# Token attention's chunks as side work of the two local-attention runs

## The chip, the cores and the metric

The kernel runs on one core of one Trainium2 chip. The metric is the device time of one execution in microseconds (us), from the chip, as the median of several runs; less is better. Engines are named as in the profile: PE (matrix products), PEld (its weight loads), DVE (vector), ACT (scalar), POOL (GpSimd), SP (which only issues DMAs here).

## The reference

The reference is a hybrid network on x of shape 8 x 256 x 128, eight residual stages one after the other, each on the layer-normed x. What matters here are stages 2 to 4:

```python
x = x + _L0_ffn_ref(_layernorm(x), Wqkv, q_scale, k_scale, Wo, ln_g, ln_b, W1, b1, W2, b2)   # stage 2: "local"
x = x + _L0_attn_b_ref(_layernorm(x), Wq, Wk, Wv, Wo, bo)                                      # stage 3: "token"
x = x + _L0_ffn_ref(_layernorm(x), Wqkv, q_scale, k_scale, Wo, ln_g, ln_b, W1, b1, W2, b2)   # stage 4: "local" again, same weights
```

The local stage is six layers of windowed attention (16 heads of 64, windows of 32 that look one window back, rotary tables, l2-normed q and k) and a gated feed-forward. Stages 2 and 4 use the same weights. The token stage is, in the reference's own words:

```python
q = (x @ Wq.T).reshape(N, S, H, hd).transpose(0, 2, 1, 3)   # N, S, D = x.shape; H = 16 heads, hd = 8
k = (x @ Wk.T).reshape(N, S, H, hd).transpose(0, 2, 1, 3)
v = (x @ Wv.T).reshape(N, S, H, hd).transpose(0, 2, 1, 3)
att = jnp.einsum('nqhd,nkhd->nhqk', q, k)
att = jax.nn.softmax(att / jnp.sqrt(jnp.asarray(hd, x.dtype)), axis=3)
```

followed by the product with v and by Wo and bo. In the kernel this stage is written for each row of 128 features as a 16 x 16 table of products, summed over 8 and soft-maxed, on DVE and POOL rather than on PE.

## The kernel before

x is held as 128 features by tokens and cut into four chunks of 512 tokens (`NCH`, `CT`). Between stages the chunks go through DRAM: `k.put(c, ...)` stores chunk c, `k.get(c, ...)` loads it, both issued on SP. One large SBUF tile `big` is divided by hand (`Arena`), and the eight PSUM banks are handed out by strings of bank numbers (`bank("01234")` takes the next of five).

**Local stage** (`LocalBlock`). A unit is one layer of one chunk, so there are 24 units, in the order layer by layer, chunk by chunk. `steps` runs a loop over i; at step i, work of several units is issued, each at a fixed distance: `project` of the pair of heads that comes 7 steps later, `rotate` 6, `prep` 1, `scores` 0, `turn` 2 back, `attend` 3 back. A unit has eight steps. Its feed-forward (`feed`, a generator) is advanced by one piece in each of steps 12 to 19 of the unit, and unit 23, the last, gets its pieces at steps 196 to 203. Scores begin at step 0 and end at step 191: steps -10 to -1 are the fill, steps 192 to 211 the drain. `end(c)` adds the residual and stores chunk c, at steps 179, 187, 195 and 203. `begin(c)` loads, norms and places chunk c for a run: chunk 0 before the loop, chunk 1 from step -10, whose load is issued at the end of that step. `side` is a list of generators that prepare the next layer's weights (`load_qk`, `load_tab`, `load_v`, `load_1`, `load_2`), one piece of each per step. `run` loads the weights of the first layer before the loop.

The whole loop stands inside `manual_schedule()`. Inside such a region each engine issues its instructions in the order in which the program emits them; where they fall among instructions from outside the region is left to the scheduler of the framework. Code outside a region is ordered by that scheduler altogether.

**Token stage** (`TokenAttention`). It is outside any such region. Each of four chunks is a `Chain` with its own place in SBUF and two PSUM banks. `chunk` is a generator: `rows` (norm), and then four tiles of 128 tokens, each in four pieces that end at a `yield`:

- A: the product for q, k, v (L1001) and its copies out of PSUM (ACT L1003, L1004);
- B: q times k on POOL (L1010), then the sum (DVE L1014), the maximum, the difference (L1016, L1018), the exponential (ACT L1019), its sum and reciprocal (L1021, L1022);
- C: the weights times v, on DVE and POOL (both L1026), the sum (DVE L1029) and the division (L1031);
- D: eight scaled copies (ACT L1035), eight products (PE L1038) and the residual (DVE L1040).

`weave` emits chunks 0 and 1 alternately, one piece behind each other, then 2 and 3; the scheduler then moves instructions as it sees fit. Chunk 0 needs only what `end(0)` stored, so some of it stands in the trace before the local run has ended.

The main loop calls the stages in turn: `local.run(depth)` for stages 2 and 4, `TokenAttention(k).run()` for stage 3.

Of the kernel before, what the change touches and what calls it, by code (L numbers as in the profile page):

```python
# [217 lines left out]
class LocalBlock:  # L218


    def __init__(self, k):
        self.k, self.nkb = k, 0
        nc = k.nc
# [52 lines left out]
    def load_v(self, w, l, g):  # L276

        k, P, nc = self.k, self.P, self.k.nc
        v, o = (self.raw(k.a[n][l, :, 4 * g:4 * g + 4], (64, 4, 128), "r" + n) for n in ("wv", "wo"))
        yield  # L280
        wp = k.bank(RING)
        for h in range(4):
            nc.tensor.matmul(wp[:, bass.ts(h, 128)], v[:, h], o[:, h], start=True, stop=True)
        wv = P.tile([128, CT], F32, name="wvo", tag="wvo", bufs=NWV)
        nc.scalar.copy(wv, wp)
        w.v.append(wv)

    def load_1(self, w, l):
        k, P, nc = self.k, self.P, self.k.nc
        w.bias1 = P.tile([128, 6], F32, name="bias1", tag="bias1", bufs=2)  # L290
        for i in (3, 4, 5, 0, 1, 2):
            m, o = (128, 128, 85)[i % 3], 341 * (i // 3) + 128 * (i % 3)
            r = self.raw(k.a["w1"][l, :, o:o + m], (128, m), "rw1")
            yield
            bp = k.bank(RING)
            nc.tensor.matmul(bp[:m, 0:1], r, self.ffc[:, l, 1:2], start=True, stop=True)
# [15 lines left out]
    def values(self, u, p):  # L312
# [6 lines left out]
        for q in range(p % 2 * 2, p % 2 * 2 + 2):  # L319
            vp = k.bank(RING)  # L320
            for w in range(4):
                win = 4 * q + w
                xw = y[:, win // 8, 32 * (win % 8):32 * (win % 8) + 32]
                for h in range(4):
                    nc.tensor.matmul(vp[32 * h:32 * h + 32, bass.ts(w, 128)], xw, wv[:, bass.ts(h, 128)],  # L325
                                     start=True, stop=True)
            nc.scalar.copy(v2[:, 4 * q:4 * q + 4].rearrange("p w f -> p (w f)"), vp)  # L327

    def project(self, u, p):
# [5 lines left out]
        for s in range(2):  # L335
            ps = k.bank(RING)
            k.mm3(ps, u.w.qk[p][:, :, bass.ts(s, 128)], u.xs)
# [52 lines left out]
    def rounded(self, u, p):  # L390
# [8 lines left out]
        u.rs[p // GP] = rs  # L399
        tp = k.bank(RING)  # L400
        nc.tensor.transpose(tp[:, 0:128], u.nr, k.ident)
# [4 lines left out]
    def prep(self, u, p):  # L406

        k, nc, tt, rs = self.k, self.k.nc, u.t[p], u.rs[p // GP]
        rb = k.bank(RING)
        nc.tensor.matmul(rb, self.bsel[:, p % GP], rs, start=True, stop=True)  # L410
# [61 lines left out]
    def turn(self, u, p):  # L472
# [6 lines left out]
        for o in range(2):  # L479
            tp = k.bank(RING)  # L480
            for wg in range(4):
# [30 lines left out]
    def attended(self, u, p):  # L512

        k, nc, ao = self.k, self.k.nc, getattr(u, "ao", None)
        if p == 7:
            tp = k.bank(RING)
# [17 lines left out]
    def feed(self, u):  # L534
        k, P, nc, w = self.k, self.P, self.k.nc, u.w
        assert u.att
        for xc, rb in k.layernorm_in_pieces(P, self.y[u.c][:, :, 0:256], (RING, RING), mid=self.mid):
            if rb is None:
# [7 lines left out]
        for i, m in enumerate((128, 128, 85)):  # L546
            gp = k.bank(RING)
            k.mm3(gp[:m], w.w1[3 + i], xh)
# [5 lines left out]
        for i, m in enumerate((128, 128, 85)):  # L554
            ap = k.bank(RING)
# [4 lines left out]
        acc = k.bank(RING)  # L560
        for i in range(3):
# [5 lines left out]
    def begin(self, c):  # L567
# [3 lines left out]
        yield  # L571
        for xc, rb in k.layernorm_in_pieces(P, xl, (RING, RING)):
            if rb is None:
# [15 lines left out]

    def run(self, depth=DEPTH):  # L590


        NU = depth * NCH
        self.P.restart()
        ws = [Rec(tab=[0, 0], qk=[], v=[], w1=[0] * 6, w2=[]) for _ in range(depth + 1)]
# [3 lines left out]
        self.mid = self.top = None  # L599
        w = ws[0]  # L600
        drain([self.begin(0)] + [self.load_tab(w, 0, n) for n in range(2)] + [self.load_v(w, 0, h) for h in range(4)] +
              [self.load_qk(w, 0, p) for p in range(8)] + [self.load_1(w, 0), self.load_2(w, 0)])
        self.mid, self.top = [], []
        with self.k.tc.manual_schedule():
            self.steps(us, ws, depth)

    def steps(self, us, ws, depth):
        NU, done, feed, side = len(us), [0] * NCH, None, []
        for i in range(-LEAD, 8 * NU + 20):
            def do(what, ahead):  # L610
                n, p = (i + ahead) // 8, (i + ahead) % 8
# [16 lines left out]
            if u:  # L628
                last = u.l + 1 == depth
                if u.c == NCH - 1 and not last:  # L630
                    side.append(self.load_qk(ws[u.l + 1], u.l + 1, p))
                    if p in (4, 5):
                        side.append(self.load_tab(ws[u.l + 1], u.l + 1, p - 4))
            do(self.norms, 6)
# [15 lines left out]
            if 0 <= n < NU and p == 7:  # L650
                u = us[n]
                next(feed)
                done[u.c] += 1
                if u.c == NCH - 1 and u.l + 1 < depth:
                    side += [self.load_1(ws[u.l + 1], u.l + 1), self.load_2(ws[u.l + 1], u.l + 1)]
# [4 lines left out]
            if u and u.c == NCH - 1 and u.l + 1 < depth and p % 2 == 0:  # L660
                side.append(self.load_v(ws[u.l + 1], u.l + 1, p // 2))
            do(self.squares, 7)
# [5 lines left out]
            if p == 0 and 0 <= n < NU:  # L668
# [287 lines left out]
class TokenAttention:  # L956
# [3 lines left out]
    def __init__(self, k):  # L960
        self.k = k
        P = Arena(k.big, TOKW)
        self.chains = [Chain(k, c, TOK[c], TOKB[c]) for c in range(NCH)]
        self.w = k.const(P, "f_w", (128, 384))
# [25 lines left out]
    def chunk(self, ch):  # L990
# [8 lines left out]
        for t in range(4):  # L999
            ps = ch.bank(0)  # L1000
            mm(ps[:, 0:384], ch.xc[:, bass.ts(t, 128)], self.w, start=True, stop=True)  # L1001
            z = ch.tile([128, 3, 128], "z", bufs=2)
            nc.scalar.activation(z.rearrange("p a f -> p (a f)"), ps[:, 0:384], AF.Copy, scale=ch.r[:, t:t + 1])  # L1003
# [349 lines left out]
def hybrid_kernel(ctx: ExitStack, tc: tile.TileContext, a, out, stages=(1, 2, 3, 4, 5, 6, 7, 8), depth=DEPTH):  # L1353
    nc = tc.nc
    k = K(ctx, tc, a)
    runs = [s for s in stages if s < 6] + [6] * (stages[-1] >= 6)
    local = None
    for s in runs:
# [141 lines left out]
```

## Time and profile before

| what | value |
|---|---|
| median of 3 runs | 4365.39 us (4363.03 to 4368.97) |
| the profiled execution | 4360.81 us, span from first to last instruction 4359.0 us |
| granted PE clock, mean | 0.926 |
| busy, of the span | PE 87%, PEld 65%, DVE 85%, ACT 60%, POOL 71% |
| scores of the first local run end | near 2187 us |
| first and last L1010 (POOL) of the token stage | start at 2205.5 and 2327.9 us |
| last store of the token stage | issued at 2362.5 us |
| first scores of the second local run | 2414.4 us |

Times in a trace are counted from the start of the span. A line of the timeline has the start, the duration, the engine, the line of the kernel, the operation and how many were merged; in square brackets stands the idle time before it and what ended it. A line of the groups has the busy time in total, then the mean in ns, and after the second bar the idle time before them. A row of the windows view has the busy time of each engine in a stretch with the number of instructions, then the clock that PE was granted (1.00 is full), the busy share of the DMA engines, and GB/s.

### The profile page before, as it was taken

How to read it: one execution, taken by the hardware profiler on the slowest of the kernel's cores; microseconds unless marked ns; L12 is line 12 of the kernel's file. 1: busy time of each engine (PE TensorE's matmuls, PEld its weight loads, DVE VectorE, ACT ScalarE, POOL GpSimd, SP SyncE). 2: the span in 40 equal slices, each digit the busy share in tenths (PEclk: the TensorE clock that was granted, in tenths of full speed). 3: DMA queues.
4: the chain of work that ended last, by engine and by line, in shares of the span. 5: the costliest groups of instructions: out<-in, count | busy, mean ns of one | idle time of the engine just before them, and what ended most of it. 6: DMA issues, size and time to landing. Idle time of an engine off the chain costs nothing. (4 is left out here: it accounts for less than half of the span.)

```text
span 4359.0 us, 147963 instructions
## 1 busy us (share of the span) xinstructions
PE 3780.3 (87%) x64201; PEld 2852.4 (65%) x64201; DVE 3716.3 (85%) x5687; ACT 2628.5 (60%) x5050; POOL 3077.8 (71%) x1546
## 2 busy tenths in 40 slices
PE   5666679999999999999966899999999999998367
PEld 2222248777878778787744788787787877875144
DVE  6999958888888888888976788888888888897988
ACT  5433347777667676676645676676676767764322
POOL 3656668877778787787566887787787877872433
PEclk7777889999999999999977999999999999998578
DMA  0000023323233233232202332232323323321000
GB/s 19 7 3 16 1 77 78 91 73 89 73 74 89 71 89 76 71 93 71 63 22 67 81 92 74 69 94 72 89 70 76 87 71 90 75 72 47 15 6 10
DMA packets 134900, 272.98 MB, mean 63 GB/s; under 512 B 31020, under 2 KB 68328, under 8 KB 134248
## 3 DMA queue, kind: packets, MB, share of 16 engines
q1 hardware_dynamic: 134248, 263.51, 24.0%
q8 instruction: 504, 8.26, 0.8%
q14 instruction: 148, 1.21, 0.1%
HBM read 49.50 MB, written 6.29 MB: 13 GB/s over the span
## 5 line engine op out<-in xcount | busy, mean ns | idle before, releaser
L367 POOL TENSOR_TENSOR big<-big 128x1024 f32<-128x1024 f32 x384 | 915.8, 2385 | 466.7 <-DMA big<-big 322.6
L368 POOL TENSOR_TENSOR big<-big 128x1024 f32<-128x1024 f32 x384 | 916.5, 2387 | 30.1
L325 PE MATMUL pb<-big 128*32 128x128 f32 x24576 | 748.1, 274 | 2.7 <-DVE big L301 2.7
L325 PEld LDWEIGHTS pb<-big 128*32 128x32 f32 x24576 | 683.0, 111 | 8.5 <-DVE big L301 4.0
L327 ACT COPY big<-pb 128x512 f32<-128x512 f32 x768 | 439.4, 597 | 384.2 <-PE pb L325 381.0
L338 ACT COPY big<-pb 128x512 f32<-128x512 f32 x768 | 437.5, 587 | 276.8 <-PE pb L215 241.7
L414 DVE SCALAR_TENSOR_TENSOR big<-big,pb 128x512 f32<-128x512 f32 x768 | 536.0, 738 | 22.3 <-PE pb L410 22.0
L340 DVE TENSOR_TENSOR big<-pb,big 128x512 f32<-128x512 f32 x768 | 496.4, 677 | 58.6 <-ACT big L338 51.5
L213 PE MATMUL pb<-bigr 128*128 128x512 f32 (+1 forms) x1056 | 453.9, 430 | 9.8 <-DVE big L340 4.3
L469 POOL TENSOR_TENSOR big<-big 128x1024 f32<-128x1024 f32 x192 | 365.6, 1904 | 132.2 <-ACT big L338 54.8
L348 ACT ACTIVATE big<-big 128x512 f32<-128x512 f32 x768 | 444.2, 631 | 0.0
L821 POOL TENSOR_TENSOR big<-big 128x1024 f32<-128x1024 f32 x128 | 305.1, 2396 | 192.1 <-DVE big L820 187.1
L429 PE MATMUL pb<-big 128*32 128x128 f32 x12288 | 421.3, 278 | 6.0 <-DVE big L440 6.0
L215 PE MATMUL pb<-bigr 128*128 128x512 f32 (+1 forms) x1056 | 422.2, 400 | 4.6 <-DVE bigr L299 4.6
L214 PE MATMUL pb<-bigr 128*128 128x512 f32 (+1 forms) x1056 | 420.9, 399 | 1.1 <-POOL bigr L203 1.1
L429 PEld LDWEIGHTS pb<-big 128*32 128x32 f32 x12288 | 316.6, 110 | 142.2 <-issue 91.2
L437 DVE TENSOR_TENSOR pb<-pb,big 128x512 f32<-128x512 f32 x384 | 266.3, 694 | 144.2 <-PE pb L429 142.6
L505 PE MATMUL pb<-big 128*32 128x128 f32 x11520 | 377.9, 276 | 0.2 <-ACT big L485 0.2
L814 PE MATMUL pb<-bigr 128*128 128x512 f32 x512 | 216.1, 538 | 181.3 <-DVE big L820 125.7
L450 ACT ACTIVATE big<-big 128x1024 f32<-128x1024 f32 x192 | 203.7, 1061 | 263.6 <-DVE big L440 261.9
L505 PEld LDWEIGHTS pb<-big 128*32 128x32 f32 x11520 | 325.1, 110 | 48.0 <-issue 25.0
L816 ACT ACTIVATE big<-pb,big 128x1020 f32<-128x1020 f32 x128 | 142.2, 1111 | 282.0 <-PE pb L814 191.1
(270 smaller groups left out, 7450.7 us busy)
## 6 DMA issues: line engine op xcount, KB each, us to landing
big<-big SPq DMA_DIRECT2D x768, 256.0 KB, 3.6
big<-in_wqk SPq DMA_DIRECT2D x96, 128.0 KB, 3.5
big<-x SPq DMA_DIRECT2D x28, 256.0 KB, 2.7
big<-in_c_rot SPq DMA_DIRECT2D x24, 256.0 KB, 5.1
big<-in_wv SPq DMA_DIRECT2D x48, 128.0 KB, 3.6
big<-in_wo SPq DMA_DIRECT2D x48, 128.0 KB, 4.0
big<-big SPq DMA_DIRECT2D x384, 16.0 KB, 2.2
x<-big SPq DMA_DIRECT2D x20, 256.0 KB, 2.5
```

Source lines behind the costliest of these rows:

```text
L213: mm(out, w[:, 0], x[:, 0], start=start, stop=False)
L215: mm(out, w[:, 1], x[:, 0], start=False, stop=stop)
L325: nc.tensor.matmul(vp[32 * h:32 * h + 32, bass.ts(w, 128)], xw, wv[:, bass.ts(h, 128)], start=True, stop=True)
L327: nc.scalar.copy(v2[:, 4 * q:4 * q + 4].rearrange("p w f -> p (w f)"), vp)
L338: nc.scalar.copy(raw[:, s], ps)
L340: nc.vector.tensor_tensor(tt[:, s].rearrange("p (b t) -> p b t", b=2), ps.rearrange("p (b t) -> p b t", b=2), ct, ALU.mult)
L348: nc.scalar.activation(sq, raw[:, s], AF.Square)
L367: nc.gpsimd.tensor_tensor(s4, s4, u.w.tab[1][:, :, None, :].broadcast_to([128, 2, 2, T]), ALU.mult)
L368: nc.gpsimd.tensor_tensor(tt, tt, sw, ALU.add)
L414: nc.vector.scalar_tensor_tensor(kb[:, h, 32:], tt[:, 1], self.hcol[:, h:h + 1], rb, ALU.mult, ALU.mult)
L429: mm(s4[32 * w:32 * w + 32, 2 * wg:2 * wg + 2], qf[:, 32 * win:32 * win + 32], kb[:, :, 32 * win:32 * win + 64].rearrange("p h (o j) -> p ...
L505: mm(u.acc[32 * w:32 * w + 32, bass.ts(wg, 128)], pts[o][:, 32 * win:32 * win + 32], v2[:, win - 1 + o], start=False, stop=(g == 3 and o = ...
```

## The change

Token attention is no longer a stage between the two local runs. Its four chunks become generators that the loop of the local stage advances. Chunks 0 and 1 are advanced by one piece per step from step 192 on (the drain of the first run), chunk 1 four steps later than chunk 0; what is left after step 211 is emitted at the end. Chunks 2 and 3 are advanced by three pieces per step in steps -10 to -3 of the second run (its fill), chunk 3 one piece behind chunk 2. All of this is now inside the two `manual_schedule()` regions.

So that the chunks fit beside the local stage, they lie in other parts of SBUF and use other PSUM banks; z and s have one buffer instead of two; the ring of banks of the local stage is four in the drain and three in the fill; the constants are loaded twice, once for each pair. The first layer's weights of the second run are now loaded during the last layer of the first (`more`), as for any other layer, and not before the second run.

```diff
-TOKW, TOK = 14880, (8880, 18160, 24160, 30160)
+TOKW, TOK = (26016, 38368), (15872, 20944, 28224, 33296)
-TOKB = (("4", "6"), ("5", "7"), ("0", "2"), ("1", "3"))
+TOKB = (("5", "6"), ("4", "7"), ("5", "7"), ("3", "4"))
-RING, SCO, NRM, ACC = "01234", "5", "6", "7"
+RING, RING_B, SCO, NRM, ACC = "01234", "0123", "5", "6", "7"
...
-    def run(self, depth=DEPTH):
+    def run(self, depth=DEPTH, more=False, ahead=(), behind=()):
-        self.P.restart()
...
+        if self.first:
+            ws[0] = self.first
+            for u in us[:NCH]:
+                u.w = ws[0]
+        else:
+            w = ws[0]
+            loads += [self.load_tab(w, 0, n) for n in range(2)] + [self.load_v(w, 0, h) for h in range(4)]
+            loads += [self.load_qk(w, 0, p) for p in range(8)] + [self.load_1(w, 0), self.load_2(w, 0)]
+        drain(loads)
...
+        self.first = ws[depth] if more else None
...
         for i in range(-LEAD, 8 * NU + 20):
+            self.ring = RING_B if i >= 8 * NU and behind else RING_B[:3] if i < -2 and ahead else RING
...
-                if u.c == NCH - 1 and not last:
-                    side.append(self.load_qk(ws[u.l + 1], u.l + 1, p))
+                if u.c == NCH - 1 and (more or u.l + 1 < depth):
+                    side.append(self.load_qk(ws[u.l + 1], (u.l + 1) % depth, p))
...
                 if n + 1 < NCH:
                     side.append(self.begin(n + 1))
                     next(side[-1])
-        assert not side
+            if i < -2:
+                for _ in range(3):
+                    ahead = [g for g in ahead if next(g, ahead) is not ahead]
+            elif i >= 8 * NU:
+                behind = [g for g in behind if next(g, behind) is not behind]
+            else:
+                assert not ahead
+        for f in self.top:
+            f()
+        self.top.clear()
+        drain(side)
+        drain(behind)
...
-            z = ch.tile([128, 3, 128], "z", bufs=2)
+            z = ch.tile([128, 3, 128], "z")
...
-            s = ch.tile([128, 16, 16], "s", bufs=2)
+            s = ch.tile([128, 16, 16], "s")
...
-    def run(self):
-        self.k.nc.scalar.preload_act_table_set("natural_log_exp_and_others")
-        for c in range(0, NCH, 2):
-            weave([self.chunk(ch) for ch in self.chains[c:c + 2]], 1)
+    def chain(self, c, skew):
+        if c % 2 == 0:
+            self.consts(TOKW[c // 2])
+        for _ in range(skew):
+            yield
+        ch = Chain(self.k, c, TOK[c], TOKB[c])
+        yield
+        yield from self.chunk(ch)
...
-            local.run(depth)
-        if s == 3:
-            TokenAttention(k).run()
+            more = s == 2 and runs[runs.index(s) + 1:][:2] == [3, 4]
+            if more:
+                token = TokenAttention(k)
+                first, second = [token.chain(0, 0), token.chain(1, 4)], [token.chain(2, 0), token.chain(3, 1)]
+            local.run(depth, more, () if more else second, first if more else ())
```

More of the change, by code (lines that the diff above doesn't have):

```diff
@@ L221, in __init__ @@
     def __init__(self, k):
-        self.k, self.nkb = k, 0
+        self.k, self.nkb, self.first = k, 0, None
         nc = k.nc
@@ L280, in load_v @@
         yield
-        wp = k.bank(RING)
+        wp = k.bank(self.ring)
         for h in range(4):
@@ L294, in load_1 @@
             yield
-            bp = k.bank(RING)
+            bp = k.bank(self.ring)
             nc.tensor.matmul(bp[:m, 0:1], r, self.ffc[:, l, 1:2], start=True, stop=True)
@@ L319, in values @@
         for q in range(p % 2 * 2, p % 2 * 2 + 2):
-            vp = k.bank(RING)
+            vp = k.bank(self.ring)
             for w in range(4):
@@ L335, in project @@
         for s in range(2):
-            ps = k.bank(RING)
+            ps = k.bank(self.ring)
             k.mm3(ps, u.w.qk[p][:, :, bass.ts(s, 128)], u.xs)
@@ L399, in rounded @@
         u.rs[p // GP] = rs
-        tp = k.bank(RING)
+        tp = k.bank(self.ring)
         nc.tensor.transpose(tp[:, 0:128], u.nr, k.ident)
@@ L408, in prep @@
         k, nc, tt, rs = self.k, self.k.nc, u.t[p], u.rs[p // GP]
-        rb = k.bank(RING)
+        rb = k.bank(self.ring)
         nc.tensor.matmul(rb, self.bsel[:, p % GP], rs, start=True, stop=True)
@@ L479, in turn @@
         for o in range(2):
-            tp = k.bank(RING)
+            tp = k.bank(self.ring)
             for wg in range(4):
@@ L515, in attended @@
         if p == 7:
-            tp = k.bank(RING)
+            tp = k.bank(self.ring)
             for wg in range(4):
@@ L536, in feed @@
         assert u.att
-        for xc, rb in k.layernorm_in_pieces(P, self.y[u.c][:, :, 0:256], (RING, RING), mid=self.mid):
+        for xc, rb in k.layernorm_in_pieces(P, self.y[u.c][:, :, 0:256], (self.ring, self.ring), mid=self.mid):
             if rb is None:
@@ L546, in feed @@
         for i, m in enumerate((128, 128, 85)):
-            gp = k.bank(RING)
+            gp = k.bank(self.ring)
             k.mm3(gp[:m], w.w1[3 + i], xh)
@@ L554, in feed @@
         for i, m in enumerate((128, 128, 85)):
-            ap = k.bank(RING)
+            ap = k.bank(self.ring)
             k.mm3(ap[:m], w.w1[i], xh)
@@ L559, in feed @@
         yield
-        acc = k.bank(RING)
+        acc = k.bank(self.ring)
         for i in range(3):
@@ L571, in begin @@
         yield
-        for xc, rb in k.layernorm_in_pieces(P, xl, (RING, RING)):
+        for xc, rb in k.layernorm_in_pieces(P, xl, (self.ring, self.ring)):
             if rb is None:
@@ L599, in run, with steps @@
         self.mid = self.top = None
-        w = ws[0]
-        drain([self.begin(0)] + [self.load_tab(w, 0, n) for n in range(2)] + [self.load_v(w, 0, h) for h in range(4)] +
-              [self.load_qk(w, 0, p) for p in range(8)] + [self.load_1(w, 0), self.load_2(w, 0)])
+        self.ring = RING
+        loads = [self.begin(0)]
+        if self.first:
[7 more added lines that the diff above has]
+        drain(loads)
         self.mid, self.top = [], []
         with self.k.tc.manual_schedule():
-            self.steps(us, ws, depth)
-    def steps(self, us, ws, depth):
+            self.steps(us, ws, depth, more, list(ahead), list(behind))
+        self.first = ws[depth] if more else None
+    def steps(self, us, ws, depth, more, ahead, behind):
         NU, done, feed, side = len(us), [0] * NCH, None, []
         for i in range(-LEAD, 8 * NU + 20):
+            self.ring = RING_B if i >= 8 * NU and behind else RING_B[:3] if i < -2 and ahead else RING
             def do(what, ahead):
@@ L628, in steps @@
             if u:
-                last = u.l + 1 == depth
-                if u.c == NCH - 1 and not last:
-                    side.append(self.load_qk(ws[u.l + 1], u.l + 1, p))
+                if u.c == NCH - 1 and (more or u.l + 1 < depth):
+                    side.append(self.load_qk(ws[u.l + 1], (u.l + 1) % depth, p))
                     if p in (4, 5):
-                        side.append(self.load_tab(ws[u.l + 1], u.l + 1, p - 4))
+                        side.append(self.load_tab(ws[u.l + 1], (u.l + 1) % depth, p - 4))
             do(self.norms, 6)
@@ L653, in steps @@
                 done[u.c] += 1
-                if u.c == NCH - 1 and u.l + 1 < depth:
-                    side += [self.load_1(ws[u.l + 1], u.l + 1), self.load_2(ws[u.l + 1], u.l + 1)]
+                if u.c == NCH - 1 and (more or u.l + 1 < depth):
+                    side += [self.load_1(ws[u.l + 1], (u.l + 1) % depth), self.load_2(ws[u.l + 1], (u.l + 1) % depth)]
                 if u.l + 1 == depth:
@@ L659, in steps @@
             u, p = do(self.values, 2)
-            if u and u.c == NCH - 1 and u.l + 1 < depth and p % 2 == 0:
-                side.append(self.load_v(ws[u.l + 1], u.l + 1, p // 2))
+            if u and u.c == NCH - 1 and (more or u.l + 1 < depth) and p % 2 == 0:
+                side.append(self.load_v(ws[u.l + 1], (u.l + 1) % depth, p // 2))
             do(self.squares, 7)
@@ L961, in __init__, with consts @@
         self.k = k
-        P = Arena(k.big, TOKW)
-        self.chains = [Chain(k, c, TOK[c], TOKB[c]) for c in range(NCH)]
+    def consts(self, at):
+        k = self.k
+        P = Arena(k.big, at)
         self.w = k.const(P, "f_w", (128, 384))
@@ L1356, in hybrid_kernel @@
     runs = [s for s in stages if s < 6] + [6] * (stages[-1] >= 6)
-    local = None
+    local, first, second = None, (), ()
     for s in runs:
```

## Prediction

> **What bounds the kernel now.** I read the page's slices first (the dip between the two local runs, near half of the span), then the windows view over that dip, the groups of instructions inside it, and the timeline. Windows view; busy us of PE, weight loads, DVE, ACT, POOL, then the granted clock:
>
> ```profile
> 2187.00:2205.00 18.00, 15.54 (x162) 11.03 (x155) 7.89 (x13) 8.80 (x15) 1.90 (x1) 0.89 0.01 2
> 2205.00:2232.00 27.00, 19.59 (x73) 12.17 (x72) 20.75 (x23) 14.31 (x31) 12.86 (x4) 0.81 0.19 59
> 2232.00:2349.00 117.00, 64.21 (x290) 50.90 (x289) 105.08 (x140) 57.19 (x175) 106.09 (x36) 0.70 0.09 29
> 2349.00:2370.00 21.00, 13.44 (x70) 10.11 (x70) 6.33 (x17) 9.39 (x25) 1.99 (x2) 0.66 0.29 87
> 2370.00:2414.40 44.40, 29.84 (x319) 20.66 (x315) 15.52 (x28) 22.36 (x46) 31.20 (x15) 0.82 0.37 93
> ```
>
> The rows are: the local drain, drain plus first token tile, the body of token attention, its tail, and the next local run's fill up to its first scores at 2414.4. In the body DVE is busy 105 and POOL 106 of 117 us: two full engines. Groups there (POOL, DVE, ACT and PE of one tile; 16 tiles):
>
> ```profile
> L1010 POOL TENSOR_TENSOR big<-big 128x2048 f32<-128x2048 f32 x16 | 72.0, 4502 | 23.2 <-ACT big L1003 23.2
> ...
> L1026 POOL TENSOR_TENSOR big<-big 128x1152 f32<-128x1152 f32 x16 | 41.8, 2612 | 1.1 <-ACT big L1019 1.1
> ...
> L1014 DVE TENSOR_REDUCE pb<-big 128x256 f32<-128x2048 f32 x16 | 36.6, 2289 | 3.8 <-POOL big L1010 3.3
> L1029 DVE TENSOR_REDUCE pb<-big 128x128 f32<-128x2048 f32 x16 | 36.5, 2282 | 4.4 <-POOL big L1026 4.2
> ```
>
> A tile needs 4.50 + 2.61 = 7.1 us of POOL. The timeline shows that the present order gets exactly that, one tile per 7.0 us (2247.49 to 2254.49 to 2261.51), POOL without a gap:
>
> ```profile
> 2247.49 4.48 POOL L1010 TENSOR_TENSOR big<-big 128x2048 f32<-128x2048 f32 x1
> 2251.93 2.61 POOL L1026 TENSOR_TENSOR big<-big 128x1152 f32<-128x1152 f32 x1
> 2254.49 4.51 POOL L1010 TENSOR_TENSOR big<-big 128x2048 f32<-128x2048 f32 x1
> 2258.95 2.62 POOL L1026 TENSOR_TENSOR big<-big 128x1152 f32<-128x1152 f32 x1
> 2261.51 4.51 POOL L1010 TENSOR_TENSOR big<-big 128x2048 f32<-128x2048 f32 x1
> ```
>
> So today's cost of the stage is engine work, overlapped across chunks by the scheduler, and the drain already hides the first tile. What the change must beat is 2414.4 - 2187 = 227 us.
>
> **What the change makes of it.** Token instructions now stand inside the two hand-ordered regions, where each engine issues in the order written. Each chunk advances one piece at a time. Call the pieces A (L1001, L1003), B (L1010 to L1022), C (L1026 to L1031), D (L1035 to L1040). No piece of a chunk's next tile is written ahead of D of the last one. A tile alone is then a chain: A 0.85 + 0.57; B 4.50 + 2.29 + 0.42 + 0.40 + 0.41; C 2.61 + 2.28 + 0.28; D 2.43 for eight L1035 and 1.95 to 3.79 for L1038: 19 to 21 us. The trace has one such tile, the first: L1010 at 2205.5, its successor at 2226.0, 20.5 us. Only two chunks are alive at a time, and two strictly serial chains can't reach 7 us per tile even if they never hinder each other (20/2 = 10).
>
> L1038 has two lengths in the timeline, after idle and after other work:
>
> ```profile
> 2254.43 3.79 PE L1038 MATMUL pb<-big 128*128 128x128 f32 x16 [4.10 <-ACT big L1035]
> ...
> 2282.66 1.97 PE L1038 MATMUL pb<-big 128*128 128x128 f32 x16
> ```
>
> *Drain, first tile.* Up to step 195 the order is nearly what the scheduler had: B of chunk 0 starts at 2205. Its L1014 stands behind unit 22's L531 and L587 (3.5 us beside POOL), so it starts at 2212.6 (before: 2211.9). Then Exp, C and D end at 2227; unit 23's norm and chunk 1's rows (L973, L980, L179, 1 us each) stand before the next A on PE: next B at 2232.5.
>
> *Drain, pairs.* Skew 4 puts both chunks in the same piece. Walk, from B of chunk 0 at 0: POOL 0 to 4.5 and 4.5 to 9.0; chunk 1's DVE part of B to 13.2; C's DVE work (1.05 + 2.2 + 0.3, twice) to 16.7 and 20.2; L1035 of chunk 1 to 22.7; L1038 (chunk 0's, cold, ended at 22.9) to 24.9; A 0.9 + 0.6: the next B at 26.4. Three such loops (steps 198 to 209) are 79. Unit 23's feed-forward is written between them: nine matmuls in step 202 stand on PE before A (+2.5), and L531 and L587 in step 203 on DVE before L1014 (+3). Its L203 waits behind two B's on POOL, and its gelu in step 200 falls into ACT's idle time before L1035: nothing; without that gap 4.6 (three L549 of 0.69 and two table loads of 1.28). Together 84.5: 2317. Then chunk 1's last tile is alone: 20, to 2337.
>
> *Handover.* SP is one queue. Region two begins by issuing the load of chunk 1 for its own norm (step -10, before the first token piece); it must wait for chunk 1's store, and chunk 2's load and four constants are queued behind it. Store 2.5, six issues of 0.33, landing 2.5, rows (2.0 + 0.5 + 1.9 + 1.0), A 0.6, some waits: 14 us. First B of chunk 2 at 2351. Part of it may be hidden, but no row shows which; bounds 6 (rows and A alone) and 18.
>
> *Fill.* Chunk 3 runs one piece behind chunk 2. Walk from B of chunk 2 at 0: POOL 4.5, C's POOL part (ready after the Exp) 8.1 to 10.75, B of chunk 3 to 15.25; its DVE part and Exp to 18.8; only then L1035 of chunk 2 (ACT has it behind that Exp) to 21.3; L1038 to 23.3 or 25; L1040 waits for it on DVE, and C of chunk 3 stands behind L1040: to 27.2 or 28.9; its L1035 29.6 or 31.4, L1038 31.6 or 35.1, L1040; chunk 2's next L1014 stands behind that last L1040 (32.0 or 35.4), and L1014 comes 4.5 after its B: loop 27.4 (both products warm) or 30.9 (both cold). I take 29.2, between them. Three loops: 87.5; the last pair to the end of its product: 35. Eight local steps lie between: where they touch the path, project's ACT work (two L338, two L348, 2.4) before L1035, two L340 behind PE and ACT (5), a rotation (L367 + L368, 4.7 on POOL, of which 1.1 shows): 8.5; if none were hidden, four projects and three rotations would be 4 x 3.8 + 3 x 4.7 = 29. End at 2351 + 131 = 2482.
>
> On the clock: the Trainium skill (TensorE: Matmul & The Clock Gate, Part 1) says that PE falls to half clock after about 3.4 us of idle and needs about as much work to recover. By that rule every product in the fill that follows a long gap would be cold, the loop 30.9 and the fill 5 us longer; the trace has cold products after gaps of only 2.1 us too (3.68 at 2310.44).
>
> *Steps -3 to 0.* Before, from L213 of step -3 (2389.0) to the first scores (2414.4): 25.4, with POOL a rotation or more behind. With the rotations caught up I take 22 (18 to 25). First scores: 2504, against 2414.4: +90.
>
> *Weights.* Run two's first weights are now loaded in run one's last layer. There the last two units' L498 are 60 us apart (read in steps of 2); with loads the same interval is 64 to 66 in every earlier layer. So 0 to 6; I take 4. What disappears between the runs (L258 loads from 2317 on, their casts and splits) lay beside the token body or in the chain I have replaced: nothing more is gained.
>
> *At nothing.* z and s lose their second buffer: the next A is written behind D anyway; if it were not, the next L1003 would wait for L1026, some 2.6. The ring of PSUM banks shrinks to four and three: a step's project takes two and L340 frees them a whole step before they return; without that slack each project would wait for an L338 and an L340, 1.3.
>
> Sum: +94. The profiled execution was 4360.8 (span 4359.0 and 1.8 around it), 4.6 under the median of 4365.4; the prediction is 4365.4 + 94 = 4459.
>
> **The rivals.**
> 1. *Perfect packing:* the two chains never hinder each other, and only their serial latency counts. From 2232.5: 3 x 19.5 + 20 + 14 + 4 x 19.5 + 3 + 22 = 2428, +4: +18, 4383. For it: engines are half idle in such a schedule. Against: the two head-of-line waits above (A behind the other chunk's D; C behind L1040). 15%.
> 2. *Faster:* the hand order does not hold back POOL. If chunk 2's pieces get into the queues while chunk 1 is still running, POOL's 148 us (154 in the five windows, less the weight splits, 8 x 0.72) run from 2205.5 without a break, to about 2352, and scores follow 10 us later (L398 at 2404.2 to 2414.4): 2362, -52, 4313. It decides only if POOL's gap per tile in the drain falls below some 3 us and chunk 2's load does not wait for chunk 1's store. The order of writing and SP's queue speak against it. 7%.
> 3. *Worse:* local steps and token pieces hinder each other in every step of the fill and the products are all cold: 20 more from the local work, 5 from the products, 8 from the drain's cold products: 4490 and above. 14%.
>
> **How the numbers follow.** Forecast 61%, 4425 to 4490. A measurement of this kernel can tell about 0.2% (9 us) from no change. Faster by more: 7% (rival 2); within: 3% (the low end of rival 1, with a shorter handover); slower: 90%. The range reaches from rival 1 to past rival 3's start: 4385 to 4505.
>
> **What would show it.** Right: successive L1010 in pairs about 4.5 apart and then a gap of 17 to 22 us; 16 of them spread over about 260 us instead of 122; POOL and DVE near half busy from 2232 to 2480; chunk 2's L973 waiting on its load after chunk 1's store; L1038 near 3.7 in the drain; first scores of run two near 2500. Wrong: L1010 every 7 to 10 us, chunk 2's B before chunk 1's last, or the dip shorter than 227 us. The handover is tested by the gap between the last L1010 of chunk 1 and the first of chunk 2 (about 34 us).

## The result and the profile after

| | before | after |
|---|---|---|
| median, same comparison | 4364.21 us (4362.54 to 4368.97) | 4465.51 us (4463.78 to 4466.69) |
| ratio | | 1.0232, 95% interval 1.022 to 1.0245 |
| span of the profiled execution | 4359.0 us | 4463.8 us |
| last group of scores (L429) of run one starts | 2184.8 | 2183.1 |
| first scores of run two | 2414.4 | 2517.6 |
| between these two ("the stretch" below) | 229.6 | 334.5 |
| from the first scores of run two to the end of the span | 1944.6 | 1946.2 |

The change made the kernel 101 us slower; 94 was predicted. All of it lies in the stretch: 334.5 - 229.6 = 104.9, against 104.8 between the spans. The stretch is read the same way in every kernel below, from the start of the last group of L429 of run one to the start of the first L429 of run two.

Token lines have moved by 23: L1010 is now L1033, L1014 L1037, L1026 L1049, L1029 L1052, L1035 L1058, L1038 L1061, L1040 L1063. Lines of the local stage up to L587 keep their numbers. The windows view, cut at the boundaries of the prediction's terms (drain; first tile; three pairs; last tile; handover; fill; last steps), and at the end the 117 us that were the full body before:

```profile
2183.10:2206.50 23.40, 19.75 (x196) 15.23 (x197) 7.08 (x12) 9.53 (x16) 1.94 (x2) 0.71 0.03 12
2206.50:2232.70 26.20, 11.87 (x54) 7.67 (x52) 13.81 (x20) 7.28 (x22) 7.12 (x3) 0.74 0.07 21
2232.70:2325.60 92.90, 34.32 (x142) 27.53 (x142) 62.15 (x73) 29.04 (x79) 43.95 (x13) 0.63 0.06 17
2325.60:2347.70 22.10, 7.34 (x34) 5.72 (x34) 9.58 (x13) 5.76 (x16) 8.30 (x3) 0.61 0.00 1
2347.70:2363.80 16.10, 6.10 (x14) 3.38 (x14) 0.38 (x2) 2.26 (x7) 0.00 (x0) 0.59 0.37 110
2363.80:2496.90 133.10, 52.74 (x259) 40.04 (x258) 68.32 (x85) 40.89 (x113) 73.64 (x24) 0.65 0.07 18
2496.90:2517.60 20.70, 16.13 (x213) 11.56 (x216) 8.12 (x15) 12.59 (x26) 14.63 (x8) 0.83 0.41 107
2232.00:2349.00 117.00, 42.22 (x178) 33.25 (x176) 71.73 (x86) 35.45 (x95) 52.28 (x16) 0.64 0.05 15
```

In the last row DVE is busy 72 of 117 us and POOL 52, where each had 105 and 106. In rows two to six no engine is busy for more than 67% (DVE, 62.15 of 92.90), and in the handover POOL does nothing at all. The groups of instructions between 2200 and 2500 show that the work is the same and what it waits for is not:

```profile
L1033 POOL TENSOR_TENSOR big<-big 128x2048 f32<-128x2048 f32 x16 | 72.0, 4506 | 108.2 <-ACT big L1026 108.2
...
L1049 POOL TENSOR_TENSOR big<-big 128x1152 f32<-128x1152 f32 x16 | 41.8, 2614 | 52.6 <-ACT big L1042 52.6
...
L1037 DVE TENSOR_REDUCE pb<-big 128x256 f32<-128x2048 f32 x16 | 36.6, 2287 | 11.5 <-POOL big L1033 11.4
```

L1033 still takes 4.51 us, sixteen times. Ahead of it POOL now idles 108.2 us, and all of that ends with L1026, the copy of piece A; before it was 23.2. The timeline of POOL has the pattern that was foretold, pairs with a hole behind each:

```profile
2206.47 4.50 POOL L1033 TENSOR_TENSOR big<-big 128x2048 f32<-128x2048 f32 x1 [13.68 <-ACT big L1026]
...
2232.67 8.92 POOL L1033 TENSOR_TENSOR big<-big 128x2048 f32<-128x2048 f32 x2 [14.05 <-ACT big L1026]
...
2262.59 9.36 POOL L1033 TENSOR_TENSOR big<-big 128x2048 f32<-128x2048 f32 x2 [14.58 <-ACT big L1026]
...
2295.43 8.91 POOL L1033 TENSOR_TENSOR big<-big 128x2048 f32<-128x2048 f32 x2 [12.29 <-ACT big L1026]
...
2325.62 4.48 POOL L1033 TENSOR_TENSOR big<-big 128x2048 f32<-128x2048 f32 x1 [14.91 <-ACT big L1026]
...
2363.82 4.48 POOL L1033 TENSOR_TENSOR big<-big 128x2048 f32<-128x2048 f32 x1 [25.48 <-ACT big L1026]
```

The starts give the terms: 2232.67 - 2206.47 = 26.2 for the first tile alone, then loops of 29.9, 32.8 and 30.2, and 38.2 from the last B of chunk 1 to the first of chunk 2.

### The profile page after: what moved, and what is told of

Its sections match the earlier page's. It is cut to its first block, busy times and chain, and to the rows that moved or that the text cites. A ratio compares the mean times of both kernels' runs of the same rounds, so it can differ in the third digit from the quotient of the medians.

```text
span 4463.8 us, 147943 instructions
## 1 busy us (share of the span) xinstructions
PE 3783.6 (85%) x64201; PEld 2854.6 (64%) x64201; DVE 3736.1 (84%) x5687; ACT 2627.6 (59%) x5050; POOL 3079.1 (69%) x1546
## 4 chain that ended last, share of the span: by engine, by line
PE 60%; DVE 21%; ACT 9%; issue 5%; POOL 2%; DMA 2%; SPq 1%; POOLq 0%; DVEq 0%; ACTq 0%
PE pb L325 11%; PE pb L505 7%; PE pb L429 6%; PE pb L213 5%; PE pb L215 4%; PE pb L214 4%; DVE big L841 4%; PE pb L359 3%; PE pb L410 3%; PE pb L563 3%; PE pb L482 3%; ACT big L338 2%; ACT big L348 2%; DVE pb L839 1%; PE pb L1061 1%
## 5 line engine op out<-in xcount | busy, mean ns | idle before, releaser
L429 PE MATMUL pb<-big 128*32 128x128 f32 x12288 | 420.0, 278 | 9.1 <-DVE big L440 9.0
L429 PEld LDWEIGHTS pb<-big 128*32 128x32 f32 x12288 | 315.7, 110 | 145.1 <-issue 90.8
```

Of the source, the lines that this page charges most:

```text
L429: mm(s4[32 * w:32 * w + 32, 2 * wg:2 * wg + 2], qf[:, 32 * win:32 * win + 32], kb[:, :, 32 * win:32 * win + 64].rearrange("p h (o j) -> p ...
```

## The experiments

Each was timed against the kernel before, except the bench at the end, which ran once; the stretch comes from the one profiled execution of each. Up to the first B the program is the same in the kernel after and in experiments 3, 4, 5, 8 and 9, and yet this part, from the last scores to the first B, took 23.3, 19.5, 23.3, 21.9, 20.3 and 19.5 us. So some 4 us of a difference between two stretches can be chance, and where it matters the part from the first B on is given too.

**1. The order.** The token stage goes back between the two runs and to the scheduler; the places in SBUF, the single buffers and the early weights stay as after (the banks as before).

```diff
-TOKB = (("5", "6"), ("4", "7"), ("5", "7"), ("3", "4"))
+TOKB = (("4", "6"), ("5", "7"), ("0", "2"), ("1", "3"))
...
-            local.run(depth, more, () if more else second, first if more else ())
+            local.run(depth, more)
+        if s == 3:
...
+            for c in (0, 2):
+                weave([token.chain(c, 0), token.chain(c + 1, 0)], 1)
...
```

> Token attention stands again between the two local runs, outside the hand-ordered regions and woven as before; what stays of the change is the rest of it: the chunks' places in SBUF, one buffer for z and s, the constants loaded twice, and the second run's first weights loaded in the first run's last layer. Theory (the written order costs the time, places and weights nothing): one L1010-type step per 7 to 8 us again, time between 4330 and 4370 us, 95 to 135 under the changed kernel. Rival (single buffers and places, or the weights in the last layer, cost it): 4420 us or more, with tiles 10 us or more apart although the scheduler orders them.

Measured: 4381.95, ratio 1.0042 (1.0027 to 1.0057); stretch 239.9. Timeline of POOL in this kernel:

```profile
2259.67 4.49 POOL L1033 TENSOR_TENSOR big<-big 128x2048 f32<-128x2048 f32 x1 [2.94 <-ACT big L1026]
...
2266.67 4.49 POOL L1033 TENSOR_TENSOR big<-big 128x2048 f32<-128x2048 f32 x1
...
2273.68 4.54 POOL L1033 TENSOR_TENSOR big<-big 128x2048 f32<-128x2048 f32 x1
```

From here six tiles come 7.0 us apart again, without a hole on POOL. The order, with the place inside the two regions and the banks that go with it, accounts for 334.5 - 239.9 = 94.6 of the 104.9. The banks and the smaller rings were not tested by themselves. The total missed its band by 12: of the 19.7 by which its span exceeds that of before, 10.3 lie in the stretch and the rest in the local runs.

**2. Places and single buffers alone.** The kernel before, with the places, single buffers and twice-loaded constants of after; its weights stay where they were.

```diff
-TOKW, TOK = 14880, (8880, 18160, 24160, 30160)
+TOKW, TOK = (26016, 38368), (15872, 20944, 28224, 33296)
...
-            z = ch.tile([128, 3, 128], "z", bufs=2)
+            z = ch.tile([128, 3, 128], "z")
...
-            s = ch.tile([128, 16, 16], "s", bufs=2)
+            s = ch.tile([128, 16, 16], "s")
...
```

> The kernel before with the changed kernel's places in SBUF, single buffers for z and s, and constants loaded twice; the banks of before, the token stage between the runs and ordered by the scheduler, weights loaded before run two as before. It shares all but the weights with the run in which the scheduler ordered the tiles (4382). Theory: the weights' preparation in the drain cost those 18 us, so this is the time of before, 4360 to 4372. Rival (places and single buffers cost it): 4378 or more.

Measured: 4378.77, ratio 1.003 (1.0018 to 1.0041); stretch 230.1. The stretch agrees with the theory: it is 0.5 longer than before, and that can be chance. By difference, experiment 1's remaining 239.9 - 230.1 = 9.8 belong to the early weights and what they meet in the drain. The total missed, and lies in the rival's band. In the profiled execution, at 4370.5 the fastest of the six, 12.2 us came before the last scores of run one (2197.0 instead of 2184.8), where the program text is that of before. I come back to this at the end.

**3. Piece A ahead of D.** In each tile, A of the next tile (now the function `head`) is written ahead of D of this one, and so ahead of the other chunk's D too.

```diff
             yield
+            if t < 3:
+                nxt = head(t + 1)
+                yield
             ex = ch.tile([128, 8, 8, 16], "ex")
...
```

> The changed kernel, but piece A of a chunk's next tile is written ahead of piece D of the tile before. Theory: A no longer waits behind the other chunk's D on PE and ACT; the next sum on DVE still stands behind both residual adds. Drain loop from 31 to about 23 us, fill loop from 30 to about 21: 3 x 8 + 3 x 9 less, 4418 us (4405 to 4435). Rival (the products' low clock or POOL and DVE work set the pace): the products' lengths stay and so does the loop, 4455 or more.

Measured: 4435.94, ratio 1.0168 (1.0153 to 1.0183); stretch 307.5, 27.0 less (23.1 from the first B on). The time is 1 us above the band, and the gain about half of the 3 x 8 + 3 x 9 = 51 from which it was worked out. The first head-of-line wait of the prediction (A behind D) is confirmed as the largest of those undone one at a time.

**4. SP's queue at the handover.** `begin`'s load of chunk 1 is written behind the token pieces of its step.

```diff
-                if n + 1 < NCH:
-                    side.append(self.begin(n + 1))
-                    next(side[-1])
...
             else:
                 assert not ahead
+            if p == 0 and 0 <= n < NU and n + 1 < NCH:
+                side.append(self.begin(n + 1))
+                next(side[-1])
```

> The changed kernel, but in step -10 the load of chunk 1 for its norm is issued after the first three token pieces, so that chunk 2's load and the constants no longer stand behind it on SP. Theory: the first q-times-k of chunk 2 comes 16 to 21 us earlier (2343 to 2348 instead of 2364), by the queue alone; 4446 us (4440 to 4452). Rival (chunk 2's start is set by the engines' queues behind chunk 1's last tile): the distance between the last q-times-k of chunk 1 and the first of chunk 2 stays at 38 us and the time at 4463 or more.

Measured: 4457.47, ratio 1.0212 (1.0195 to 1.0228); stretch 320.7, 13.8 less. First the queue in the kernel after, then POOL in this one:

```profile
2347.68 0.32 SPq L184 DMA_DIRECT2D x<-big  x1
2349.75 0.32 SPq L119 DMA_DIRECT2D big<-x  x1
2350.12 0.43 SPq L188 DMA_DIRECT2D big<-in_f_w  x1
...
2352.01 0.91 SPq L119 DMA_DIRECT2D big<-x  x2
...
2357.01 2.08 PE L996 MATMUL pb<-big 128*128 128x512 f32 x2 [9.75 <-DMA big<-x]
```

```profile
2330.84 4.48 POOL L1033 TENSOR_TENSOR big<-big 128x2048 f32<-128x2048 f32 x1 [14.91 <-ACT big L1026]
...
2355.88 4.49 POOL L1033 TENSOR_TENSOR big<-big 128x2048 f32<-128x2048 f32 x1 [12.26 <-ACT big L1026]
```

After: the store of chunk 1 (L184, 2347.68), then the load that waits for it (2349.75), then the constants and chunk 2's load (2352.01), and L996 gets its data at 2357. With the load moved, chunk 2's first B follows the last B of chunk 1 by 25.0 us instead of 38.2. What is left is chunk 1's last tile (22.0 in the kernel after) and 3 more. The cause is the one expected, the gain some 2 to 7 us smaller, and the total 5 us above its band.

**5. The residual later.** L1063 of a tile is written behind the next tile's B, so that it does not stand ahead of the other chunk's C on DVE.

```diff
-            nc.vector.scalar_tensor_tensor(xt, yp.rearrange("p i a -> p a i"), self.bo, xt, ALU.add, ALU.add)
+            late.append((xt, yp))
...
             nc.vector.reciprocal(den, den)
+            residual()
...
```

> The changed kernel, but the residual add of a tile is written after piece B of the next tile (after the last tile: before the store). Theory: in the fill C of chunk 3 no longer stands behind chunk 2's residual add on DVE, so the fill loop falls from 30 to about 27; in the drain both residual adds lie beside work that does not wait for them, 0 to -1 per loop. 4454 us (4446 to 4460). Rival (this add is not on the path): 4463 or more.

Measured: 4459.14, ratio 1.022 (1.0203 to 1.0237); stretch 323.7, 10.8 less (9.3 from the first B on, of which 8.4 lie between the first and the last B of the fill). What it took away, in the timeline of DVE of the kernel after:

```profile
2383.36 0.25 DVE L1045 RECIPROCAL big<-big 128x16 f32<-128x16 f32 x1
2389.09 0.35 DVE L1063 SCALAR_TENSOR_TENSOR big<-pb,big 128x128 f32<-128x128 f32 x1 [5.47 <-PE pb L1061]
2389.36 1.08 DVE L1049 TENSOR_TENSOR big<-big,pb 128x896 f32<-128x896 f32 x1
```

Chunk 3's L1049 could have begun at 2383.6; chunk 2's residual ahead of it waited 5.47 us for the product. This is the second head-of-line wait of the prediction (C behind L1040).

**6. The three together.**

> The changed kernel with the three reorderings at once: the next tile's piece A ahead of D, the residual add behind the next B, chunk 2's load ahead of chunk 1's. Theory (three separate head-of-line waits): their single gains add up but for the overlap of the first two, 30 + 4 + 8 = 42: 4423 us (4415 to 4432). Rival (each frees the same wait): no better than 4436.

Measured: 4424.75, ratio 1.0137 (1.0123 to 1.015); stretch 289.4, 45.1 less, where the three alone sum to 51.6 (from the first B on, 42.1 against 46.2). The time is inside its band. The three causes are nearly independent.

**7. Two pieces per tile.** One piece is B with the last tile's products, the other C, residual, next A and the scaled copies; skew 5 in the drain, two passes per step in the fill, and the load of experiment 4. The lines that cut the tile in two are left out here.

```diff
...
-                for _ in range(3):
+                for _ in range(2):
...
-                first, second = [token.chain(0, 0), token.chain(1, 4)], [token.chain(2, 0), token.chain(3, 1)]
+                first, second = [token.chain(0, 0), token.chain(1, 5)], [token.chain(2, 0), token.chain(3, 1)]
...
```

> The changed kernel, still hand-ordered in drain and fill, but a tile has two pieces, B (then the products of the tile before) and C (then that tile's residual add, the next A and L1035-type copies); chunk 1 is an odd number of pieces behind chunk 0; chunk 2's load stands ahead of chunk 1's; two pieces per step in the fill. Theory (the written order, not the placing beside the local runs, costs the time): two tiles per 17 to 20 us instead of 30, first scores of run two near 2421, 4372 us (4350 to 4392). Rival (two chunks beside local work can't do better than about 25 us per pair): 4420 or more.

Measured: 4425.14, ratio 1.0138 (1.0123 to 1.0152); stretch 279.7. It gained 9.7 on experiment 6 in the stretch and lost it again in the local runs (1958.2 from run two's first scores on, instead of 1950.0). POOL at its handover and at the end of its fill:

```profile
2313.31 4.47 POOL L1050 TENSOR_TENSOR big<-big 128x2048 f32<-128x2048 f32 x1 [4.72 <-DVE pb L1070]
...
2345.45 4.48 POOL L1050 TENSOR_TENSOR big<-big 128x2048 f32<-128x2048 f32 x1 [4.52 <-ACT big L1026]
...
2418.65 4.52 POOL L1050 TENSOR_TENSOR big<-big 128x2048 f32<-128x2048 f32 x1
```

The eight B's of the fill are spread over 2418.65 - 2345.45 = 73.2 us (after: 108.7), about 21 per pair where POOL's own work is 14.2; but 32.1 us lie between the last B of chunk 1 and the first of chunk 2, which had been 25.0 in experiment 4. In the drain nothing was gained: its eight B's are spread over 105.8 us (experiment 6: 103.0). My expectation of 4350 to 4392 fell, and the total lies in the rival's band (4420 or more). Products and sums of one chunk share a PSUM bank, and local feed-forward work stands between the pieces; which of these holds it most was not separated.

**8. Half of the products.** To see whether the cold L1061 lie on the path.

```diff
-            for d in range(8):
-                mm(yp, self.wo[:, d], ex[:, :, d], start=(d == 0), stop=(d == 7))
+            for d in range(4):
+                mm(yp, self.wo[:, d], ex[:, :, d], start=(d == 0), stop=(d == 3))
```

> The kernel after, but each token tile makes only four of its eight L1061 products (the other half of the output projection is left out, so the values are not the reference's; every other instruction stays). Theory (the tiles are a chain of latencies, and the cold products lie on it): of the kernel after, one tile's eight products took 3.2 to 3.8 us cold, two tiles' 6.41 in a drain loop; with half of them the first tile gives back 1.7, three drain loops 3.2 each, the last tile 1.7, three fill loops 3.3 each, the last pair 3.3: 26 in all, so the stretch from run one's last scores to run two's first scores is 308 (302 to 314) instead of 334.5 and the time some 4440 (4434 to 4447). Rival (the products lie beside DVE and POOL work, and the loops are set by those): the stretch shrinks by 0 to 6, the time stays at 4459 to 4466.

Measured: 4458.38, ratio 1.0224 (1.0204 to 1.0244); stretch 316.3, 18.2 less, between the two expectations, and not evenly: the fill's three loops and last pair gave 11.6 of the expected 13.2, the three drain loops 0.8 of the expected 9.6, and 3.0 came before the first B, where nothing had changed. The timeline of the second drain loop, PE alone, first after, then with half of the products:

```profile
2287.39 6.41 PE L1061 MATMUL pb<-big 128*128 128x128 f32 x32 [11.49 <-ACT big L1058]
...
2293.78 1.54 PE L1024 MATMUL pb<-big 128*128 128x384 f32 x4
```

```profile
2282.73 2.08 PE L1061 MATMUL pb<-big 128*128 128x128 f32 x8 [11.71 <-ACT big L1058]
...
2286.45 2.07 PE L1061 MATMUL pb<-big 128*128 128x128 f32 x8 [1.64 <-ACT big L1058]
...
2288.60 2.91 PE L1024 MATMUL pb<-big 128*128 128x384 f32 x4
```

With half the products the second tile's product waits 1.64 us for its scaled copies (L1058), and the next A, which has to run straight behind, takes 2.91 instead of 1.54: PE was granted less clock (0.57 over the three loops, 0.63 in after). That it was granted less because it had done less is likely, but was not tested by itself. In the drain the products were only just the last to arrive.

**9. The weights of the feed-forward out of the drain.** `load_1` of run two's first layer runs before run two.

```diff
-                    side += [self.load_1(ws[u.l + 1], (u.l + 1) % depth), self.load_2(ws[u.l + 1], (u.l + 1) % depth)]
+                    nx = (u.l + 1) % depth
+                    side += ([self.load_1(ws[u.l + 1], nx)] if nx else []) + [self.load_2(ws[u.l + 1], nx)]
...
+            loads.append(self.load_1(ws[0], 0))
```

> The changed kernel, but the second run's first feed-forward weights (load_1, six pieces that fall into steps 204 to 209) are prepared before run two instead. Theory: two of its L299 on DVE are stretched to 3.1 and 2.2 us beside POOL and stand on the drain's path, with smaller hand-offs around them: 5 to 8 less in the drain, 0 to 6 more ahead of run two; 4462 us (4455 to 4467). Rival (they are off the path): 4466 to 4472.

Measured: 4488.51, ratio 1.028 (1.026 to 1.0299); stretch 333.7. From the last scores to chunk 1's last B it was 5.0 us shorter (137.5 instead of 142.5), but 3.8 of these lie before the first B, ahead of any piece of `load_1`. The third drain loop, in which both long L299 stand, took 27.3 instead of 30.2, the first 31.0 instead of 29.9. The handover was 3.1 longer, the rest up to run two's first scores 1.2. So `load_1` costs the drain some 3 us at most, less than the 5 to 8 expected, and moving it gained nothing in sum. The total is above both bands and inconclusive: of the 24.7 us between the two profiled executions, 19.8 lie in run two after its first scores and 5.6 before the last scores of run one.

**10. DVE beside POOL, by itself.** In the traces above some short DVE instructions are very long. The timeline of DVE in the drain of the kernel after:

```profile
2266.66 5.84 DVE L587 TENSOR_TENSOR big<-big 64x512 f32<-64x512 f32 x2
...
2294.11 0.34 DVE L299 SCALAR_TENSOR_TENSOR bigr<-big,bigr 128x128 fp32r<-128x128 f32 x1
2296.91 3.09 DVE L299 SCALAR_TENSOR_TENSOR bigr<-big,bigr 128x85 fp32r<-128x85 f32 x1 [2.39 <-ACT bigr L298]
...
2308.69 2.17 DVE L299 SCALAR_TENSOR_TENSOR bigr<-big,bigr 128x128 fp32r<-128x128 f32 x1
```

A bench repeats the forms, alone and beside POOL:

```python
for f in (two, wide, small, one, red):                                   # DVE alone
    phase(b_pool, 0, f, 8)
for f, n in ((two, 12), (wide, 12), (small, 16), (one, 20), (red, 6)):   # beside L1033's form
    phase(b_pool, 5, f, n)
for f, n in ((two, 12), (small, 16)):                                    # beside L1049's form
    phase(c_pool, 8, f, n)
```

> Not the network: a bench of its own that leaves all of the computation out and only repeats the instructions of the case, first POOL alone (the forms of L1033 and L1049, six each), then DVE alone (eight each: the two-input add of L587, 64x512 and 128x512; the L299 form, 128x128, two inputs from SBUF; a 128x512 product with one input from PSUM, as L325; the 2048-element sum of L1037), then the same DVE forms beside back-to-back L1033, and two of them beside L1049. Theory (the two engines share a way to SBUF, and DVE pays when it reads two operands from there): the two-input forms are 2.5 to 8 times as long beside L1033 as alone (0.69 to 1.8 or more for 64x512, 0.34 to 2 or more for 128x128), the PSUM form and the sum stay within 10%, and L1033 stays at 4.50 throughout. Rival (the long L587 and L299 of the kernel after came from something else, such as the DMA or PE traffic of that moment): all DVE forms keep their lengths within 15%.

Measured, groups of the bench (line numbers are its own): L1554 is 128x512 with two inputs from SBUF, first alone, then in the 24 us beside L1543, the form of L1033; then L1557 (the form of L299) beside it; and L1560, with one input from PSUM, beside it:

```profile
L1554 DVE TENSOR_TENSOR big<-big 128x512 f32<-128x512 f32 x8 | 5.5, 692 | 2.3 <-ACT big L1576 2.0
```

```profile
L1554 DVE TENSOR_TENSOR big<-big 128x512 f32<-128x512 f32 x5 | 23.8, 4767 | 2.2 <-ACT big L1576 2.1
```

```profile
L1543 POOL TENSOR_TENSOR big<-big 128x2048 f32<-128x2048 f32 x5 | 22.3, 4466 | 7.7 <-ACT big L1574 7.4
L1557 DVE SCALAR_TENSOR_TENSOR big<-big 128x128 f32<-128x128 f32 x5 | 22.3, 4454 | 2.3 <-ACT pb L1575 2.1
```

```profile
L1560 DVE TENSOR_TENSOR big<-pb,big 128x512 f32<-128x512 f32 x20 | 13.8, 691 | 2.5 <-ACT big L1576 1.8
```

Exactly one DVE instruction of these two forms gets done per POOL instruction, whether it takes 0.69 or 0.29 alone. Beside the 2.60 us form of L1049, the 64x512 add took 2.92; beside L1033's form only two of its twelve overlapped POOL. The form with a PSUM input (0.691) and the sum of 2048 (2.295 throughout) did not notice POOL. The theory that DVE pays holds, and more sharply than expected: it is not slowed down, it waits. Each of these DVE instructions ends 0.1 to 0.6 us behind the end of a POOL instruction. POOL pays a little too, against the expectation: beside the 128x512 form its instructions took up to 4.79 instead of 4.47.

## Why the prediction was right, point by point

| term | predicted | measured |
|---|---|---|
| second tile's B starts | 2232.5 | 2232.7 |
| three drain loops | 84.5 | 92.9 |
| last tile of chunk 1 | 20 | 22.0 |
| handover | 14 | 16.2 |
| fill to the last product | 131 | 133.0 |
| steps -3 to 0 | 22 | 20.7 |
| first scores of run two | 2504 | 2517.6 |
| weights, in run one's last layer (distance of the last two L498) | +4 | +2.1, not shown to be theirs |

*The mechanism.* Two chains, each serial by the order of writing, with POOL waiting for A: the 108.2 us of idle time before L1033 and experiment 1 show it. Both head-of-line waits that the prediction named are real, worth 27.0 and 10.8 of the stretch by themselves. The first row agrees in part by luck: the first B came 1.5 us late (2206.5 for 2205), and the tile behind it took 26.2 for 27.5. The signs that it named came as well: the 16 B's are spread over 266 us (named: 260), and 38.2 lie between the last B of chunk 1 and the first of chunk 2 (named: 34).

*Drain loops, 8.4 too short: the mis-sized term.* Loop by loop the prediction had 28.9, 29.4 and 26.4; measured 29.9, 32.8, 30.2. In each loop it counted chunk 1's product warm; the two together took 6.88, 6.41 and 6.86 instead of 3.8 + 2.0, some 0.6 to 1.1 each. In the second, the two L587 took 5.84 where they had taken 3.54 before, so that chunk 0's L1037 began 9.9 after B and not 7.5: 2.4. In the third, the L299 at 2308.69 with its L301 pushed the C of chunk 0 by 2.3; the prediction had costed the weights' work in the drain at nothing, and experiment 9, without it there, has a third loop that is 2.9 shorter. Some 4 of the 8.4 us are what experiment 10 isolates. The other long L299 (2296.91) ended at 2300.0, when L1037 had to wait for L1033 anyway, and cost nothing. The row of before:

```profile
2207.75 3.54 DVE L587 TENSOR_TENSOR big<-big 64x512 f32<-64x512 f32 x2
```

The Trainium skill (SBUF — State Buffer, section "Who interferes with whom") says that a DVE instruction with two SBUF inputs and a POOL instruction that reads SBUF exclude each other, and that the later one stands until the earlier ends. The bench's 4.77 and 4.45 us agree. The prediction took the 3.5 us of before as L587's price beside POOL; read with that rule, that row is a wait that depends on where POOL is, and two adds beside two L1033 in a row can't end before the second does (here it ended at 2271.95, they at 2272.50).

*Fill: right in sum, by two errors that cancel.* Counted from B to B its loops were 28.2, 31.8 and 31.0, and the last pair took 42.0. But the walk takes its loop from one L1014 (now L1037) to the next; B starts ahead of that, and L1037 then waits behind the residual adds. Chunk 2's L1037 in the first, the second and the last tile:

```profile
2368.42 2.29 DVE L1037 TENSOR_REDUCE pb<-big 128x256 f32<-128x2048 f32 x1
...
2399.78 2.29 DVE L1037 TENSOR_REDUCE pb<-big 128x256 f32<-128x2048 f32 x1
...
2466.18 2.28 DVE L1037 TENSOR_REDUCE pb<-big 128x256 f32<-128x2048 f32 x1
```

The first loop, which has no `project` and no rotation in it, took 31.4 (walk, cold: 30.9), the other two 66.4. From the last of these rows to the end of the last product it is 30.7 (walk: 35 less 4.5, which is 30.5). So the walk itself held, and two of its terms were mis-sized. Local work showed as some 5 us (97.8 less 3 x 30.9) where 8.5 stood. And the products were cold in every loop, not in half of them, which is 1.7 more in each loop:

```profile
2385.27 3.79 PE L1061 MATMUL pb<-big 128*128 128x128 f32 x16 [14.69 <-ACT big L1058]
2395.69 3.78 PE L1061 MATMUL pb<-big 128*128 128x128 f32 x16 [4.47 <-ACT big L1058]
...
2493.44 3.42 PE L1061 MATMUL pb<-big 128*128 128x128 f32 x16 [2.94 <-ACT big L1058]
```

The prediction had set the 3.4 us rule of the Trainium skill (TensorE: Matmul & The Clock Gate, Part 1) against a middle value; the rule's side was nearer. It is not the gap just ahead alone that decides, though: products were cold behind 2.94 and 1.67 us of idle too (the second, 3.74 long, at 2418.62), and experiment 8 shows PE at a lower clock when it had fewer products.

*Handover.* 16.2 for 14; experiment 4 shows that some 13 of it were SP's queue.

*Weights.* The last two L498 of run one, by whose distance the prediction sized this term, are 63.2 us apart instead of 61.1. That lies within its 0 to 6, but in experiment 2, which loads no weights there, they are 66.0 apart, and the last scores of the kernel after even came earlier (2183.1 instead of 2184.8). So a cost in this layer is not shown. By difference, experiments 1 and 2 place some 10 us in the stretch, where the prediction had put nothing.

*At nothing.* Under the scheduler's order the stretch with single buffers is 0.5 longer (experiment 2), which can be chance; under the hand order they were not tested alone.

*The rivals.* Perfect packing needs chains that never hinder each other; experiments 3 and 5 price how much they do. The faster rival needs chunk 2's pieces in POOL's queue while chunk 1 runs: POOL has 25.48 us of idle time before chunk 2's first B. The worse rival was right on cold products in every loop; but the local work in the fill cost less than predicted and not 20 us more, and its 33 us were too many.

*What stays open.* Experiments 3 to 5, put together in experiment 6, explain 45.1 of the 94.6 us that the order costs; how the other 49.5 divide among cold products, local work between the pieces, the coarse pieces and the banks was not settled, and experiment 7 did not recover them. Of all versions none beat the kernel before: the nearest were experiments 2 (4378.8) and 1 (4382.0), both with the scheduler's order.

## What to carry to other kernels

Work that fills two engines to 90% can get slower as side work, as here, even if its place looks idle: what was overlapped across tiles became a chain of latencies. Such a chain should be added up (here 20 us per tile against 7.1 of engine time) before work is moved. In a fixed order, look on each engine for the instruction that waits while a ready one of another chain stands behind it, SP's queue included. When several such waits are found, undo them one at a time: here they added up to within 15%.

## What the runs showed of the hardware that was not expected

- Beside POOL's `tensor_tensor`, a DVE instruction with two inputs from SBUF goes from 0.69 or 0.29 us to 4.77 and 4.45: one per POOL instruction. With one input in PSUM it stays at 0.691. In the kernel before, DVE's share of L1026, which reads v from PSUM, fits this: it takes 1.08 us each of 16 times, once beside the L1010 of POOL that starts at 2254.49:

```profile
2254.53 1.08 DVE L1026 TENSOR_TENSOR big<-big,pb 128x896 f32<-128x896 f32 x1
```

- Behind fewer matrix products the next ones were slower: L1024's four records took 2.91 us instead of 1.54 behind half of the products.
- The local runs differ by more than their edits can say. From the first scores of run two to the end, the kernels took 1941.6 (experiment 2) to 1966.0 us (experiment 9), and the last scores of run one started between 2180.6 and 2197.0, with nearly the same program there. The cause was not found. Differences of some 10 us between totals of this kernel should not be read without the stretch they come from.
